# Gate and up of a fused AdaLN block on one core: from 2x2 block products of one pair to a 26-product 4x4 by 4x2 scheme over two pairs

## The chip, the cores and the metric

One core of one Trainium2 chip runs the whole program in one launch. The metric is device time in microseconds (us) of that core, and the time of a kernel is the median of its runs. Of the kernel before there are three: 2610.93, 2619.89 and 2622.31 us, so the median is 2619.89 us.

## The reference, cut to what matters

x is 2 x 2048 x 1024 and the feed-forward width is 2752. The attention is across the two batch entries only, so it is cheap; nearly all arithmetic lies in the three weight matrices.

```python
h = layernorm(x) * (1 + ca) + sa
x = x + ga * attention_over_the_2_batch_entries(h)
h = layernorm(x) * (1 + cb) + sb
gate = silu(h @ W_gate.T)       # W_gate, W_up: 2752 x 1024
up = h @ W_up.T
x = x + gb * ((gate * up) @ W_down.T)   # W_down: 1024 x 2752
```

## The kernel before, in words

**Tiling.** The tokens are cut into eight units of 2 x 256 (512 columns). A unit runs in three stages. *Gate and up* makes H = silu(gate) * up, 21 blocks of 128 rows and one of 64, taken as ten pairs of blocks (p = 0 to 9), a single block (p = 10) and a left-over of 64 rows (`gu_left_over`, L1034). *Down* multiplies by W_down in seven steps of 120 matmuls (L1166). Then eight groups of five matmuls add the last rows of W_down (`pB`, L1196). `unit` does one unit; the loop at the end of the program does eight.

**Precision.** An f32 operand is held as two f16 parts, high and low. A product is three matmuls (`PARTS`): high by high, high by low, low by high. `split` makes the two parts: ScalarE writes the high one (L168), VectorE the low one (L172), as source times scale minus high. Scales are powers of two found from sums of squares (L151).

**Fewer products.** Gate-and-up of one pair is a 2x2 by 2x2 block product: rows are gate and up, the inner side is two halves of the 1024 inputs, columns are the two batch entries. `gu_pair` (L996) does it in 7 products in place of 8, after Strassen and Winograd, in the order `GU_STEPS`, with three PSUM accumulators X, Y, Z, each in two buffers. VectorE and ScalarE put the results together: L1001, L1004, L1007, L1010, L1013, L1014, L1016, L1018, L1019, L1022, L1023. `gu_as_is` (L964) does the 8 plain products. The seven left operands of a pair are sums of its four weight blocks.

**Where left operands are built.** The first unit uses plain f16 blocks (`gu_plain`, L939, matmuls of 512 columns) and stores them to DRAM (`dgu`). In the second unit the odd pairs and p = 10, in the third the even pairs, are built from f32 weights loaded again (`Stream`, `operand`; sums at L447 to L452) and used at once, and stored for later. The even pairs run plain in the second unit. From the fourth unit on all seven operands are loaded from `dgu`.

**Right operands.** `right_gu` makes eight right operands of the next unit's h (four blocks, four sums) with copies of 1024 columns on ScalarE (L899) and sums on VectorE (L900 to L913), beside the last three down steps.

**The next unit's h.** `prep(u + 1)` is a generator (`side`): loads, attention, layer norm. Its VectorE lines are L687, L688, L703, L704, L706, L713, L719, L159 to L162 and L731. GpSimd sums over partitions twice in it (L694). `unit` calls it between steps.

**What sets the order.** Loads and stores are issued by SyncE, in one queue. Engines work in order. From the second unit on a list scheduler lays out each engine's order when the program is built; it moves instructions of all engines, matmuls too, where their operands allow it. `tc.issue_after` and the places of the `yield`s hold it back. PSUM has eight banks: X, Y, Z twice, and two for small things. `rot` (five blocks of 1024 columns) holds the right operands of two down steps in turn, and in the second and third units also the f32 weights that operands are built from.

**Other lines that are spoken of.** L166 is a high part made by GpSimd, and L132 a maximum over partitions on GpSimd; both are in the first unit. L841 is a sum of 512 columns on GpSimd before the first unit.

Of the kernel before, what the change touches and what calls it, by code (L numbers as in the profile page):

```python
# [16 lines left out]
P = 128  # L17
# [22 lines left out]
GU_STEPS = (("X", 1), ("Y", 6), ("Z", 5), ("X", 2), ("Y", 7), ("Z", 3), ("Y", 4))  # L40
DN_STEPS = (("X", 1), ("Z", 5), ("Y", 6), ("X", 2), ("Y", 7), ("Z", 3), ("Y", 4))
LAST = ((0, 0, 0), (0, 0, 1), (0, 1, 0), (1, 0, 0), (1, 1, 0))
PARTS = ((0, 0), (0, 1), (1, 0))
# [3 lines left out]
def adaln_kernel(ctx, tc, x, xT, wgp, wg20, wgl, wd, wd20, wd21, wmod, cT, out, nunits=NU):  # L47
# [23 lines left out]
    ets = {"sil": [0, 1], "e1": [2, 3], "e5": [4]}  # L71
    bct = ct([P, 2, 2, TU], "bct")
    hb = hbt.bitcast(F16).rearrange("p (o h k c) -> p o h k c", o=8, h=2, k=4)
    rot16 = rot.bitcast(F16).rearrange("p (s h k c) -> p s h k c", s=2, h=2, k=KH)
    zt = big[:, 2].rearrange("p (k n c) -> p k n c", k=KB, n=2)
    flat = lambda t: t.rearrange("p a b -> p (a b)")

    def et_tile(tag):

        i = ets[tag].pop(0)  # L80
        ets[tag].append(i)
        return mix[:, 3 * D + i * 2 * TU:3 * D + (i + 1) * 2 * TU].rearrange("p (n c) -> p n c", n=2)
# [291 lines left out]
    def x_step(s, between):  # L374
# [32 lines left out]
        for n in range(2):  # L407
# [10 lines left out]
    AS_IS = range(0, NP, 2)  # L418
    PAIRS = {1: list(range(NP + 1)), 2: [p ^ 1 for p in range(NP)] + [NP]}
    BUILT = {1: [p for p in PAIRS[1] if p not in AS_IS], 2: list(AS_IS)}  # L420
    dgu = {(p, i): dr.tile([P, 2 * min(2, NF - 2 * p) * 4 * P], F16, tag=f"dgu{p}_{i}", name=f"dgu{p}_{i}")
           for p in range(NP + 1) for i in range(0 if p in AS_IS else 1, 8)}
# [9 lines left out]

    ORDER = [i for _, i in GU_STEPS]
    BLOCKS = (1, 2, 0, 4)
    PLAIN = {1: 0, 2: 1, 4: 3}
    AHEAD0, AHEAD1 = 3, 4
# [18 lines left out]
    class Pair:  # L455
# [49 lines left out]
        def store(self, i, w):  # L505
            if i != 2 or self.p in AS_IS:
                Q.dma_start(dgu[self.p, BLOCKS[i]], w)

        def operand(self, i):
            w = self.w[i] = wtile(2 * self.n, "wo")  # L510
            split(w[:, 0:self.n], w[:, self.n:], combine(self.q, i), self.s)
            Q.dma_start(dgu[self.p, i], w)

    class Stream:


        def __init__(self, u):
            self.items = [(p, i) for p in PAIRS[u] for i in (range(4) if self.as_is(u, p) else ORDER)]
            self.u, self.to_build, self.w, self.n, self.src = u, list(BUILT[u]), {}, 0, {}
            self.at = 0  # L520

        @staticmethod
        def as_is(u, p):
            return u == 1 and p in AS_IS

        def next_source(self):
            if self.to_build:
                p = self.to_build.pop(0)
                self.src[p] = Pair(p, ring(self.n))
                self.n += 1  # L530
                self.src[p].load()

        def make(self, k):
            while self.at <= min(k, len(self.items) - 1):
                p, i = self.items[self.at]
                self.at += 1
                if p in BUILT[self.u] and i not in PLAIN:
                    self.src[p].operand(i)
                    self.w[p, i] = self.src[p].w.pop(i)
                    if i == 3:  # L540
                        self.next_source()
                else:
                    w = self.w[p, i] = wtile(2 * min(2, NF - 2 * p) * 4 * P, "wo")
                    Q.dma_start(w, dgu[p, BLOCKS[i] if self.as_is(self.u, p) else i])

    NXT = 3
    FROM, EVERY = 8, {1: 2, 2: 2}
# [11 lines left out]

    def ring(p):  # L560

        at = lambda j: rot[:, j % 6 * D:(j % 6 + 1) * D] if j % 6 < 5 else hpf
        return [at(4 * p + j) for j in (0, 3, 1, 2)]
# [329 lines left out]


    def right_gu(E):
        b11, b12, b21, b22 = (zt[:, 4 * i:4 * i + 4, n] for i in range(2) for n in range(2))

        def op(i, src):
            S.copy(hb[:, i, 0], src)  # L899
            V.tensor_tensor(hb[:, i, 1], src, hb[:, i, 0], ALU.subtract)  # L900

        op(1, b11)
        E.tensor_tensor(b11, b12, b11, ALU.subtract)
        yield
        op(5, b11)
        E.tensor_tensor(b11, b22, b11, ALU.subtract)
        yield
        op(6, b11)
        op(2, b21)
        yield  # L910
        E.tensor_tensor(b21, b21, b11, ALU.subtract)
        op(0, b12)
        E.tensor_tensor(b12, b22, b12, ALU.subtract)  # L913
        yield
        op(7, b12)
        op(3, b22)
        yield
        op(4, b21)
        yield
# [32 lines left out]
    def gu_as_is(p, ws, asq, tick):  # L952

        inv = inv_f[:, p:p + 1]
        pt = {(m, f): ps.tile([P, 2, TU], F32, tag="XYZ"[(4 * p + 2 * m + f) % 3], name=f"g{m}{f}")
              for m in range(2) for f in range(2)}
        for i in range(4):
            m, kh = i // 2, i % 2
            w = ws(i).rearrange("p (h f k c) -> p h f k c", h=2, f=2, k=4)
            for f in range(2):  # L960
                for k in range(4):
                    for j, (wa, ha) in enumerate(PARTS):
                        for n in range(2):
                            T.matmul(pt[m, f][:, n], w[:, wa, f, k], hb[:, ((1, 0), (2, 3))[kh][n], ha, k],  # L964
                                     start=kh == 0 and k == 0 and j == 0 and n == 0,
                                     stop=kh == 1 and k == 3 and j == 2, skip_group_check=True)
            if kh:
                for f in range(2):
                    if m == 0:
                        sil = evp.tile([P, 2, TU], F32, tag="ev", name="silp", bufs=3)  # L970
                        S.activation(sil, pt[m, f], AF.Silu, scale=inv)
                        pt["s", f] = sil
                    else:
                        mark["pair", p] = V.scalar_tensor_tensor(H[:, 2 * p + f], pt[m, f], inv, pt["s", f], ALU.mult, ALU.mult)
            tick(i)
        sumsq(H[:, 2 * p:2 * p + 2].rearrange("p f n c -> p (f n c)"), asq[:, p:p + 1])
# [7 lines left out]
    def gu_pair(u, p, ws, asq, tick):  # L984
        nf = min(2, NF - 2 * p)
        acc = {a: ps.tile([P, 2, TU], F32, tag=a, name=f"p{a}") for a in "XYZ"}
        pt = {a: acc[a][:, 0:nf] for a in "XYZ"}
        inv = inv_f[:, p:p + 1]
        et = lambda tag: (evp.tile([P, 2, TU], F32, tag=tag, name=tag, bufs=3) if tag == "ev" else et_tile(tag))[:, 0:nf]
        seen = set()  # L990
        for si, (a, i) in enumerate(GU_STEPS):
            w = ws(i).rearrange("p (h f k c) -> p h f k c", h=2, f=nf, k=4)
            for f in range(nf):
                for k in range(4):
                    for j, (wa, ha) in enumerate(PARTS):
                        T.matmul(pt[a][:, f], w[:, wa, f, k], hb[:, i, ha, k], start=a not in seen,  # L996
                                 stop=k == 3 and j == 2, skip_group_check=True)
                        seen.add(a)
            if si == 0:
                e1 = et("e1")  # L1000
                S.copy(e1, pt["X"])  # L1001
            if si == 1:
                u2 = et("ev")
                V.tensor_tensor(u2, pt["Y"], e1, ALU.add)  # L1004
            if si == 2:
                e5 = et("e5")
                S.copy(e5, pt["Z"])  # L1007
            if si == 3:
                sl = et("sil")
                S.activation(sl, pt["X"], AF.Silu, scale=inv)  # L1010
            if si == 4:
                c22 = et("ev")
                V.tensor_tensor(c22, pt["Y"], e1, ALU.add)  # L1013
                V.tensor_tensor(c22, c22, e5, ALU.add)  # L1014
            if si == 5:
                V.tensor_tensor(u2, pt["Z"], u2, ALU.add)  # L1016
                sr = et("sil")
                S.activation(sr, u2, AF.Silu, scale=inv)  # L1018
                V.scalar_tensor_tensor(H[:, 2 * p:2 * p + nf, 1], c22, inv, sr, ALU.mult, ALU.mult)  # L1019
            if si == 6:  # L1020
                c21 = et("ev")
                V.tensor_tensor(c21, pt["Y"], e1, ALU.add)  # L1022
                mark["pair", p] = V.scalar_tensor_tensor(H[:, 2 * p:2 * p + nf, 0], c21, inv, sl, ALU.mult, ALU.mult)  # L1023
            tick(si)
        sumsq(H[:, 2 * p:2 * p + nf].rearrange("p f n c -> p (f n c)"), asq[:, p:p + 1])

    def gu_left_over(u, w, asq, between=lambda: None):
        pl = ps.tile([P, 2, TU], F32, tag="X", name="pl")
        w = w.rearrange("p (h k c) -> p h k c", h=2, k=KB)
        for n in range(2 if u else 1):  # L1030
            for k in range(KB):
                o = ((1, 0), (2, 3))[k // 4][n]
                for j, (wa, ha) in enumerate(PARTS):
                    T.matmul(pl[:, n] if u else pl.rearrange("p n c -> p (n c)"), w[:, wa, k],  # L1034
                             hb[:, o, ha, k % 4] if u else hb0[:, ha, k], start=n == 0 and k == 0 and j == 0,
# [3 lines left out]
        sl = et_tile("sil")  # L1039
# [7 lines left out]
    def unit(u, side, nxt):  # L1047
# [34 lines left out]
        taken, before = 0, None  # L1082
        for p in PAIRS.get(u, range(NP + 1)):
            if u == 0:
# [7 lines left out]
            elif u in streams:  # L1092
                st = streams[u]

                def tick(si):
                    nonlocal taken
                    taken += 1
                    st.make(taken + AHEAD1)
# [510 lines left out]
```

## Time and profile before, and how to read it

| | |
|---|---|
| median of three runs | 2619.89 us |
| the profiled execution: time | 2618.47 us |
| its span, first to last instruction | 2616.3 us |
| TensorE, share of the span | 97% |
| VectorE, ScalarE, GpSimd | 61%, 37%, 4% |
| DMA | 586.61 MB, mean 224 GB/s |
| start of the last-rows stage (`pB`) of the eight units | 465.7, 791.0, 1097.9, 1397.9, 1701.5, 2001.8, 2305.0, 2603.9 us |

Units are numbered 1 to 8 here. The time from one `pB` to the next is one unit: its `pB`, then gate-and-up and down of the following one. So 465.7 to 791.0 is the period of the second unit (325.3 us), and so on. In a row of groups the two numbers after the bar are busy time in us and mean length of one in ns; then follow the idle time ahead of it and what ended that. A line of the timeline has start, length, engine, line, operation; "x2" are two instructions in a row.

### The profile page before, as it was taken

The page shows a single profiled execution, that of the slowest core. Times are in us where ns is not written, and L with a number is a line of the kernel's source. Part 1 is how long each engine was busy: PE and PEld are TensorE (multiplying, and loading weights), DVE is VectorE, ACT ScalarE, POOL GpSimd, SP SyncE. Part 2 cuts the span into 40 slices and gives each one's busy share as a digit, 9 for nine tenths or more (in the row PEclk, how much of TensorE's full clock was granted, in tenths as well). Part 3 has the DMA queues.
Part 4 walks back from the last instruction along what each step waited for, and adds up shares of the span by engine and source line. Part 5 has one row for each costly group of instructions (what it writes and reads, how often), then busy time and mean ns, then how long its engine had stood idle before and what let it go on. Part 6 is the DMA issues. An engine that isn't in the chain of part 4 may idle for free.

```text
span 2616.3 us, 50450 instructions
## 1 busy us (share of the span) xinstructions
PE 2543.5 (97%) x21699; PEld 2089.9 (80%) x21699; DVE 1588.7 (61%) x2616; ACT 978.8 (37%) x1402; POOL 114.1 (4%) x68
## 2 busy tenths in 40 slices
PE   7899969999999999999999999999999999999999
PEld 3344448788887888888887888888887888888887
DVE  8778697565767777592376625584284725622263
ACT  7667764233432454152241423233141412311231
POOL 6200000000000000000000000000000000000000
PEclk9999989999999999999999999999999999999999
DMA  9978756755568766676666666676666666666664
GB/s 391 395 282 317 290 205 207 263 171 199 176 214 286 262 214 211 204 232 202 200 200 226 201 202 200 197 237 201 186 219 219 198 201 200 202 197 202 202 203 156
DMA packets 154976, 586.61 MB, mean 224 GB/s; under 512 B 16768, under 2 KB 16832, under 8 KB 154752
## 3 DMA queue, kind: packets, MB, share of 16 engines
q1 hardware_dynamic: 154752, 583.38, 67.3%
q8 instruction: 170, 2.79, 0.4%
q14 instruction: 54, 0.44, 0.1%
HBM read 506.47 MB, written 76.84 MB: 223 GB/s over the span
## 4 chain that ended last, share of the span: by engine, by line
PE 81%; DMA 7%; DVE 6%; ACT 2%; issue 2%; POOL 0%; SPq 0%; DVEq 0%; ACTq 0%; POOLq 0%
PE pY L996 19%; PE pZ L996 12%; PE dY L1166 12%; PE pX L996 12%; PE dZ L1166 8%; PE dX L1166 8%; PE g L964 3%; PE g L939 2%; PE pB L1196 2%; DMA wo<-dgu 1%; PE pl L1034 1%; DMA out_dram<-big 1%; DVE bst L289 1%; DMA rot<-in_wgp_dram 1%; DMA wl<-dgl 1%
## 5 line engine op out<-in xcount | busy, mean ns | idle before, releaser
L996 PEld LDWEIGHTS <-w 128*128 128x128 f16 x8820 | 864.2, 98 | 113.0 <-DMA w<-dgu 8.3
L1166 PEld LDWEIGHTS <-wd 128*128 128x128 f16 x6720 | 658.2, 98 | 82.2 <-issue 5.6
L996 PE MATMUL pY<-hbt,w 128*128 128x256 f16 x3780 | 444.0, 273 | 0.0
L1166 PE MATMUL dY<-rot,wd 128*128 128x256 f16 x2880 | 318.6, 273 | 0.0
L996 PE MATMUL pZ<-hbt,w 128*128 128x256 f16 x2520 | 295.9, 273 | 7.2 <-DMA w<-dgu 7.2
L996 PE MATMUL pX<-hbt,w 128*128 128x256 f16 x2520 | 300.6, 273 | 0.0
L996 PEld LDWEIGHTS <-wo 128*128 128x128 f16 x2688 | 263.9, 98 | 41.7 <-DMA wo<-dgu 7.4
L168 ACT ACTIVATE rot<-H,sA 128x1024 f16<-128x1024 f32 x168 | 162.3, 1001 | 235.7 <-PE dY L1166 126.9
L172 DVE SCALAR_TENSOR_TENSOR rot<-H,sA,rot 128x1024 f16<-128x1024 f32 x168 | 182.7, 1101 | 81.9 <-ACT rot L168 81.5
L939 PE MATMUL g<-hbt,wq 128*128 128x512 f16 x1008 | 221.1, 381 | 8.3 <-DVE wq L172 3.6
L1166 PE MATMUL dX<-rot,wd 128*128 128x256 f16 x1920 | 214.7, 274 | 4.9 <-issue 4.9
L1166 PE MATMUL dZ<-rot,wd 128*128 128x256 f16 x1920 | 214.7, 273 | 0.1
L1013 DVE TENSOR_TENSOR ev<-pY,mix 128x512 f32<-128x512 f32 (+1 forms) x72 | 47.8, 663 | 257.8 <-PE pY L996 256.7
L939 PEld LDWEIGHTS <-wq 128*128 128x128 f16 x1008 | 98.3, 98 | 132.5 <-issue 7.5
L151 ACT ACTIVATE junk<-H 128x1024 bf16<-128x1024 f32 (+1 forms) x102 | 100.8, 988 | 177.5 <-DVE H L1023 149.6
L1018 ACT ACTIVATE mix<-ev,inv_f 128x512 f32<-128x512 f32 (+1 forms) x72 | 50.4, 701 | 248.2 <-DVE ev L1016 247.6
L996 PE MATMUL pY<-hbt,wo 128*128 128x256 f16 x1152 | 135.8, 274 | 2.7 <-DMA wo<-dgu 1.3
L702 ACT ACTIVATE o<-big,beta,alpha 128x256 f32<-128x256 f32 x96 | 51.5, 593 | 194.8 <-DVE big L688 181.7
L1004 DVE TENSOR_TENSOR ev<-pY,mix 128x512 f32<-128x512 f32 (+1 forms) x72 | 47.7, 662 | 123.9 <-PE pY L996 123.9
L1007 ACT COPY mix<-pZ 128x512 f32<-128x512 f32 (+1 forms) x72 | 40.4, 561 | 190.6 <-PE pZ L996 190.6
L1147 DVE SCALAR_TENSOR_TENSOR big<-dY,cA,big 128x256 f32<-128x256 f32 x96 | 41.9, 478 | 113.7 <-PE dY L1166 113.7
L964 PE MATMUL g<-hbt,wo 128*128 128x256 f16 x960 | 108.1, 275 | 2.3 <-DMA wo<-dgu 2.3
(331 smaller groups left out, 2734.4 us busy)
## 6 DMA issues: line engine op xcount, KB each, us to landing
w<-dgu SPq DMA_DIRECT2D x350, 512.0 KB, 4.2
wd<-dwd SPq DMA_DIRECT2D x224, 640.0 KB, 5.1
wo<-dgu SPq DMA_DIRECT2D x85, 512.0 KB, 5.4
dgu<-wo SPq DMA_DIRECT2D x40, 512.0 KB, 3.9
rot<-in_wgp_dram SPq DMA_DIRECT2D x38, 512.0 KB, 5.9
dgu<-wq SPq DMA_DIRECT2D x35, 512.0 KB, 6.5
dwd<-hbt SPq DMA_DIRECT2D x28, 640.0 KB, 3.3
out_dram<-big SPq DMA_DIRECT2D x30, 512.0 KB, 3.8
```

The lines of the kernel that those rows point to most:

```text
L151: S.activation(jv, src, AF.Square, accum_out=col)
L168: mark["hi"] = S.activation(dst_hi, src, AF.Copy, scale=s)
L172: return V.scalar_tensor_tensor(dst_lo, src, s, dst_hi, ALU.mult, ALU.subtract)
L702: S.activation(o[:, n], z[:, q, 0], AF.Identity, scale=alpha[:, n, 0, q:q + 1], bias=beta[:, n, q:q + 1])
L939: T.matmul(pt[m, f].rearrange("p n c -> p (n c)"), w[:, wa, f, k], hb0[:, ha, 4 * kh + k], start=kh == 0 and k == 0 and j == 0, stop=kh == ...
L964: T.matmul(pt[m, f][:, n], w[:, wa, f, k], hb[:, ((1, 0), (2, 3))[kh][n], ha, k], start=kh == 0 and k == 0 and j == 0 and n == 0, stop=kh ...
L996: T.matmul(pt[a][:, f], w[:, wa, f, k], hb[:, i, ha, k], start=a not in seen, stop=k == 3 and j == 2, skip_group_check=True)
L1004: V.tensor_tensor(u2, pt["Y"], e1, ALU.add)
L1013: V.tensor_tensor(c22, pt["Y"], e1, ALU.add)
L1018: S.activation(sr, u2, AF.Silu, scale=inv)
L1166: T.matmul(acc[a, h][:, j], w[:, k // 5, wa, k % 5], rot16[:, si % 2, ha, k], start=(a, h) not in seen, stop=k == KH - 1 and jj == 2, skip ...
L1196: T.matmul(pB, wt[:, k, wa, m, :], hp[:, k, ha, :], start=i == 0, stop=i == len(LAST) - 1)
```

## The change

- The first unit stores all four plain blocks of every pair (before, the third block of the odd pairs and of p = 10 was not stored).
- The second unit does all ten pairs plain (`gu_as_is`), and p = 10 too. Beside it a generator, `build`, makes the left operands of all five groups of two pairs: per group 35 sums of 512 columns, two of three on GpSimd and the third on VectorE, and 26 splits of 512 columns, each stored to DRAM (`dq`, 256 KB). It loads all f32 weights again. Its f32 blocks lie in `rot` and in the second half of `hbt`, 16 registers of 512 columns and one more, and three for temporary sums; the f16 results use five places in `mix`.
- From the third unit on `gu_group` does two pairs at a time: gate and up of two pairs are four rows, the 1024 inputs four quarters, the batch entries two columns. 26 products of 2 x 2 x 3 matmuls stand in place of 2 x 7 products of 2 x 4 x 3. It uses six accumulators (all six banks of X, Y, Z), 22 sums and 4 products on VectorE and 6 copies and 4 silu on ScalarE in each group. p = 10 runs plain.
- `right_gu` makes 27 right operands of 512 columns with 21 sums (in the second unit the 8 plain ones). They lie in `hbt`, in `rot` (ten places, those of the two down buffers) and in one block of H.
- `Feed` loads left operands four tiles ahead, in their order of use, 512 KB each. `prep` is called at each tile in the second unit and at every fifth later.

The core of the diff:

```diff
-GU_STEPS = (("X", 1), ("Y", 6), ("Z", 5), ("X", 2), ("Y", 7), ("Z", 3), ("Y", 4))
+G_STEPS = (
+    (2, 4, True, (('c', 0),)),
+    (10, 2, True, (('c', 1),)),
+    (12, 3, True, (('c', 2),)),
+    (17, 4, False, (('+', 1, 1),)),
...
+    (19, 5, False, (('-', 2, 2), ('h', 2, 0, 0, 1),)),
+)
+G_LEFT = (
+    ('e', 13, 1, 1), ('e', 12, 4, 1), ('e', 17, 10, 1), ('o', 't', 12, '-', 0), ('e', 15, 't', 1),
+    ('o', 0, 0, '+', 1), ('o', 12, 12, '-', 0), ('o', 't', 0, '-', 10), ('e', 2, 't', 1), ('o', 't', 12, '+', 9),
...
+)
+    def build():
...
+        for i in range(8):
+            load(0, i)
+        nt = ns = na = 0
+        for q in range(NQ):
+            last = None
+            for at, x in enumerate(G_LEFT):
+                reg = lambda r: last if r == "t" else regs[r]
+                if x[0] == "o":
...
+                    na += 1
+                    E = V if na % 3 == 0 else G
+                    E.tensor_tensor(dst, reg(a), reg(b), ALU.add if sign == "+" else ALU.subtract)
...
+                    w = place(ns % 5).bitcast(F16).rearrange("p (h f c) -> p h f c", h=2, f=2)
+                    s = s_q[:, int(sign < 0), q:q + 1]
+                    split(w[:, 0], w[:, 1], reg(src), s)
+                    j = at_of[r]
+                    Q.dma_start(dq[q, j // 2][:, j % 2 * NL:(j % 2 + 1) * NL], w.rearrange("p h f c -> p (h f c)"))
+                for i, e in ends.items():
+                    if e == at and q + 1 < NQ:
+                        load(q + 1, i)
+                if x[0] == "e":
+                    yield
...
+    def gu_group(q, take, asq, tick):
+        inv = inv_q[:, q:q + 1]
+        acc = [ps.tile([P, 2, TU], F32, tag="XYZ"[i % 3], name=f"p{i}") for i in range(6)]
+        e = [place(i).rearrange("p (f c) -> p f c", f=2) for i in range(5)]
+        e.append(evp.tile([P, 2, TU], F32, tag="ev", name="e", bufs=3))
+        for at, (r, a, first, reads) in enumerate(G_STEPS):
+            if at % 2 == 0:
+                w2 = take().rearrange("p (t h f k c) -> p t h f k c", t=2, h=2, f=2, k=2)
+            w, right = w2[:, at % 2], right_of(G_OPERAND[r])
+            for f in range(2):
+                for k in range(2):
                     for j, (wa, ha) in enumerate(PARTS):
+                        T.matmul(acc[a][:, f], w[:, wa, f, k], right[:, ha, k], start=first and f == 0 and k == 0 and j == 0,
+                                 stop=k == 1 and j == 2, skip_group_check=True)
+            for x in reads:
+                if x[0] == "c":
+                    S.copy(e[x[1]], acc[a])
...
+                else:
+                    sign, src, dst = x
+                    in0, in1 = (acc[a], e[src]) if sign == "r" else (e[src], acc[a])
+                    V.tensor_tensor(e[dst], in0, in1, ALU.add if sign == "+" else ALU.subtract)
+            tick()
...
+        def tick(*_):
+            nonlocal taken
+            taken += 1
+            if u == 1:
+                for _ in range(3 + taken % 3 // 2):
+                    run_gen(builder)
+                if taken > 5:
+                    run_gen(side)
+            elif taken % 5 == 0:
+                run_gen(side)
...
+            if u == 1:
+                builder = build()
+                for p in range(NP):
+                    gu_as_is(p, feed.take, asq, tick)
+                for _ in builder:
+                    pass
             else:
+                for q in range(NQ):
+                    gu_group(q, feed.take, asq, tick)
+            close_scale(0, 0, NP)
+            gu_as_is(NP, feed.take, asq, tick)
...
-                if si >= 4:
-                    with tc.issue_after(mark["lo", NXT].ins), tc.issue_after(mark["hi", NXT].ins):
-                        run_gen(nxt)
-                        run_gen(nxt)
+                if si >= READY:
+                    with tc.issue_after(mark["lo", READY].ins), tc.issue_after(mark["hi", READY].ins):
+                        for _ in range((5, 6, 5, 5)[si - READY]):
+                            run_gen(nxt)
```

## The prediction

> **What bounds the kernel now.** First the page: busy time, the slices, the chain.
>
> ```profile
> PE 2543.5 (97%) x21699; PEld 2089.9 (80%) x21699; DVE 1588.7 (61%) x2616; ACT 978.8 (37%) x1402; POOL 114.1 (4%) x68
> ...
> DVE  8778697565767777592376625584284725622263
> ...
> PE 81%; DMA 7%; DVE 6%; ACT 2%; issue 2%; POOL 0%; SPq 0%; DVEq 0%; ACTq 0%; POOLq 0%
> ```
>
> TensorE is never free for long and makes 81% of the chain; VectorE swings between 2 and 9 tenths. Then the stretches from one `pB` to the next, one unit each (columns: stretch, its length, busy time of PE, weight loads, DVE, ACT, POOL, clock, DMA share, GB/s), and one piece of the chain.
>
> ```profile
> 465.70:791.00 325.30, 316.99 (x2818) 277.36 (x2817) 207.47 (x300) 111.47 (x161) 6.48 (x2) 0.98 0.61 204
> 791.00:1097.90 306.90, 301.31 (x2698) 264.31 (x2696) 215.28 (x317) 116.09 (x167) 6.47 (x2) 0.99 0.70 236
> 1097.90:1397.90 300.00, 298.98 (x2698) 263.73 (x2697) 171.13 (x277) 94.66 (x147) 6.47 (x2) 1.00 0.67 208
> ...
> 2305.00:2603.90 298.90, 298.80 (x2698) 263.76 (x2696) 111.33 (x179) 62.99 (x94) 0.00 (x0) 1.00 0.62 193
> ```
>
> ```profile
> 2551.52 13.10 PE dX L1166 x120
> ```
>
> 120 matmuls of 256 columns take 13.10 us: 0.1092 us each, 0.2184 for 512 columns. A unit from the third on has 1764 + 48 + 840 of them and 40 of 512 columns: 2652 x 0.1092 + 8.7 = **298.3 us**, against 298.9 to 306.9 measured. Only fewer matmuls can shorten such a unit. The second has 1884 in place of 1764: 311.4, so 13.9 of its 325.3 are idle.
>
> **Matmuls.** From the third unit on, 10 pairs x 168 + 84 become 5 groups x 26 x 12 + 96 = 1656: 108 fewer, 11.8 us; the floor is 286.5 us. Six units: -70.8. The second goes from 1884 to 10 x 192 + 96 = 2016: +14.4, floor 325.9. TensorE alone would save 56.4 us.
>
> **The build in the second unit.** Five groups x 35 sums are 175, of which 117 fall to GpSimd and 58 to VectorE; 130 splits. Prices:
>
> ```profile
> L841 POOL TENSOR_TENSOR big<-o,big 128x512 f32<-128x512 f32 x5 | 6.3, 1274 | 3.2 <-DVE o L840 3.2
> ```
>
> ```profile
> 1144.56 4.90 DVE L713 TENSOR_TENSOR big<-big,mean 128x512 f32<-128x512 f32 x8
> ...
> 1170.22 6.41 DVE L731 SCALAR_TENSOR_TENSOR big<-big,b1s,r 128x256 f32<-128x256 f32 x16
> ```
>
> ```profile
> 1326.99 1.40 DVE L172 SCALAR_TENSOR_TENSOR mix<-H,sA,mix 128x512 f16<-128x512 f32 x2
> ```
>
> In a row, VectorE takes 0.61 us for a sum of 512, 0.40 for the 256-column form, 0.70 for a split. So GpSimd: 117 x 1.274 = 149.1, and 2 x 3.2 for the sums over partitions = **155.5**. VectorE: 130 x 0.70 + 58 x 0.61 = 126.4; `prep` 46 x 0.61 + 32 x 0.40 + 2 = 42.9; together **169.3**, plus 21 plain results x 0.745 = 15.6. Either fits beside TensorE's 225.4 us (2016 + 48 matmuls). Whether both do depends on what happens when they meet. Four lines of one place, GpSimd and VectorE side by side:
>
> ```profile
> 134.05 1.12 POOL L166 TENSOR_SCALAR wq<-rot,s_gu 128x1024 f16<-128x1024 f32 x1 [18.62 <-DVE inv_gu L139]
> 135.81 1.49 POOL L166 TENSOR_SCALAR wq<-rot,s_gu 128x1024 f16<-128x1024 f32 x1 [0.64 <-DMA dgu<-wq]
> ```
>
> ```profile
> 135.02 3.34 DVE L172 SCALAR_TENSOR_TENSOR wq<-rot,s_gu,wq 128x1024 f16<-128x1024 f32 x2 [0.91 <-ACT wq L168]
> 138.64 1.28 DVE L172 SCALAR_TENSOR_TENSOR wq<-rot,s_gu,wq 128x1024 f16<-128x1024 f32 x1 [0.27 <-ACT wq L168]
> ```
>
> Alone, the GpSimd instruction takes 1.12 and two splits 2 x 1.28 less an overlap of 0.08 = 2.48. Overlapping, they take 1.49 and 3.34: GpSimd loses 0.37, VectorE 0.86 us. Likewise a VectorE sum meets the sum over partitions here:
>
> ```profile
> 1139.65 3.23 POOL L694 PARTITION_ALL_REDUCE mean<-acc  x1 [210.07 <-DVE acc L706]
> ...
> 1140.47 1.98 DVE L1014 TENSOR_TENSOR ev<-ev,mix 128x512 f32<-128x512 f32 x1
> ```
>
> 1.98 in place of about 0.69. In both, VectorE reads two operands from SBUF. L841's neighbours (L840) read one from PSUM, and L841 keeps 1.27. Splits, VectorE's sums and `prep` all read two from SBUF. If such an instruction and a GpSimd one exclude each other, the two totals add: 155.5 + 169.3 = **325 us**, 99 over TensorE. If GpSimd only holds VectorE up for 0.86 of its 1.12 (77%), 117 x 1.274 x 0.77 = 115, and the sum is 290. If they don't hinder each other, 225.4 and the 13.9 idle us of before. I take 325: the lines with two SBUF operands are the ones like the build's.
>
> The Trainium skill, "GPSIMD Engine Reference", section Specifications, says that GpSimd's SBUF interfaces are shared with VectorE, with contention from VectorE instructions that have two SBUF inputs. By L841's row alone this stage would last 225 us; by the page's rule, read as exclusion, 325; no run here shows a long series of both.
>
> Upper bound: add four changes of GpSimd's work between plain sums and sums over partitions, in a program with both (its first p2g waited 6.5 us for nothing that the profile shows: 26 us), and four reloads of f32 blocks between groups, since a group's last steps use blocks that the next group's first steps want (5.9 us median to landing, 24 us): 375.
>
> TensorE can't run away from it: VectorE works in order and writes H between the build's instructions, and the first down operand overwrites the build's `rot`. That operand (L168, L172: 1.15 + 1.28) is then late by some 3 us. Second unit: 325 + 3 + 91.7 (down) + 8.7 = **428, +103** over 325.3. Ends: +14 (225.4 + 13.9 + 100.4 = 339.7) and +153.
>
> DMA: 80 MB (21 plain blocks, 21 f32, 34 stores, the rest small), 247 GB/s over 325 us, against 391 in the page's densest slices; at 225 us it would be 356 and no longer loose. Stores queue ahead of weights on SyncE, but four loaded tiles are 4 x 48 x 0.109 = 21 us ahead.
>
> **Third to eighth unit.** VectorE gets 5 x (22 + 4) results, 16.4 us a group (22 x 0.61 + 4 x 0.745), and 48 steps for right operands, 29.3 us, for 14.6 before (12 x 1.22, the row of L900). In the down stage VectorE sat idle for most of 1361 to 1398, which takes the latter; the last few wait for `rot` and fall into the first group, which doesn't need them at once. In the groups, the built program's order puts nearly all of `prep` (42.9 and reciprocals 3.4) into the first two: 2 x 16.4 + 41 (less 5.3 that stand earlier) = 73.8 us beside 2 x 34.1 = 68.2 of matmuls. All six accumulators are one group's; where VectorE lags, TensorE waits. I take 5 us for the difference and 5 for the next group's first copies, which stand behind the last products and the sums of squares (1.06 each) on ScalarE: **10 us** idle. Ends: 1.7 (the third to seventh stretch's best) and 20 (`prep` at the rows' means, 0.69 and 0.48, and once more the 5). The eighth has no `prep`: 4.
>
> Third: 296.5 - 306.9 = -10.4. Fourth to seventh: 4 x 296.5 - 1207.1 = -21.1. Eighth: 290.5 - 298.9 = -8.4. Sum **-40**; ends -84 and +10.
>
> **At nothing.** The first unit's 6 more stores (under 4 MB beside half-idle DMA; 2 us if the cover is gone), its shorter right operands (-9 us of VectorE off the path), the scales (a few 0.15 us).
>
> **Sum**, against the profiled execution (2618.5: its span and 2.2 us around it that stay; 1.4 below the median): 2618.5 + 103 - 40 = **2682 us**. If the build's sum is 290: 2647. With everything at its upper end: 2618.5 + 153 + 10 = 2782; at its lower: 2618.5 + 14 - 84 = 2549.
>
> **Rivals.**
> - *Faster: the build hides.* GpSimd and VectorE share without loss, each 70 to 85% busy, and gate-and-up of the second unit stays at 239. For it: each total is below 225.4, and L841. 2618.5 + 14 - 40 = **2593**; with the best idle times 2549. It decides from a build under 262 us, where +40 in the second unit equals the -40 later.
> - *About the same: exclusion in part.* Some meetings cost, splits go on while GpSimd waits for a sum of VectorE; build 265 to 275: +43 to +53, -40: **2627**.
> - *Slower still: the order binds.* One group's 61 steps are a chain, GpSimd waits for VectorE's third sum and both for reloaded blocks; build 375: +153, -40, so **2732**, and to 2782 if the groups also starve.
> - That the product isn't done as said is excluded: the built program has 516 matmuls fewer, 132 x 1 - 108 x 6.
>
> **How the numbers follow.** Forecast (build 290 to 350) 0.60; hidden 0.18; in part 0.11; order binds 0.11. The range reaches down to the hidden case's 2593 and up past 2732: 2590 to 2745, with about 0.09 below and 0.06 above. By half a per cent (about what a measurement here can tell from no change), faster is below 2606.8 (0.18), the same up to 2633 (0.10), slower above (0.72). The likeliest case's own range is 2647 to 2707.
>
> **What would show it.** Right: gate-and-up of the second unit near 325 us, with TensorE waiting for VectorE's results there; GpSimd sums and VectorE splits longer than 1.27 and 0.75 where they overlap; later periods near 296 us; each later idle gap ended by VectorE or ScalarE at a group's border. Wrong: overlapping sums and splits at their lone lengths, a second unit near 340 us, or later periods that don't fall below 300.

## The result, and the profile after

The changed kernel takes **2708.66 us**, the median of four runs (2704.33 to 2718.33), against 2615.41 us for the kernel before in the same measurement: ratio 1.0363, 95% interval 1.0317 to 1.0409. It is slower, and the forecast of 2682 was 27 us too low. The profiled execution took 2718.33 us, 9.7 above the median; its span is 2716.5.

From its page, busy time, the slices of GpSimd, the granted clock (in tenths of full speed) and the chain:

```profile
PE 2522.0 (93%) x21183; PEld 2050.5 (75%) x21183; DVE 1970.7 (73%) x3224; ACT 1080.0 (40%) x1631; POOL 305.6 (11%) x185
...
POOL 6200100536750010001000010001000000000000
PEclk9999989988879999999999999999999999999999
...
PE 58%; DMA 7%; DVE 5%; POOL 2%; issue 2%; ACT 1%; POOLq 0%; SPq 0%; DVEq 0%; ACTq 0%
```

TensorE issues 516 matmuls fewer and is busy 21 us less, but its share of the span falls from 97% to 93%. GpSimd is busy in five slices of the second unit, and there TensorE's granted clock is lowest. The stretches from one `pB` to the next (second, third and eighth unit):

```profile
466.30:903.30 437.00, 349.71 (x2951) 297.70 (x2950) 356.02 (x437) 172.50 (x268) 194.19 (x119) 0.90 0.65 224
903.30:1205.90 302.60, 291.53 (x2589) 254.41 (x2587) 219.88 (x368) 106.19 (x173) 6.80 (x2) 0.99 0.57 195
...
2414.80:2703.90 289.10, 287.55 (x2590) 252.98 (x2588) 149.42 (x240) 68.83 (x104) 0.00 (x0) 1.00 0.55 188
```

The periods of all units, in us, from the start of one `pB` to that of the next in each profiled execution. The columns e1 to e9 are experiments, told of below; those of e5, e8 and e10 that matter are given there.

| unit | before | after | e1 | e2 | e3 | e4 | e7 | e9 |
|---|---|---|---|---|---|---|---|---|
| 2 | 325.3 | 436.9 | 387.7 | 451.9 | 435.4 | 389.6 | 341.9 | 341.5 |
| 3 | 306.9 | 302.7 | 301.3 | 303.3 | 290.7 | 294.1 | 302.7 | 300.9 |
| 4 | 300.0 | 301.8 | 302.4 | 301.7 | 291.7 | 294.0 | 294.1 | 292.5 |
| 5 | 303.4 | 302.9 | 302.7 | 303.0 | 292.4 | 295.0 | 294.3 | 291.1 |
| 6 | 300.3 | 301.0 | 300.2 | 303.8 | 291.3 | 294.7 | 296.5 | 293.2 |
| 7 | 303.3 | 303.1 | 300.1 | 303.5 | 291.1 | 292.7 | 294.1 | 290.1 |
| 8 | 298.9 | 289.1 | 289.3 | 288.7 | 288.7 | 288.7 | 289.6 | 288.8 |

Two things happened. The second unit grew by 111.6 us. And of the six units that have fewer matmuls, only the eighth, the one in which no next h is made, became shorter as its matmuls did (-9.8); the five between gained 2.4 us together.

**The second unit.** Groups of GpSimd and VectorE in its gate-and-up:

```profile
L644 POOL TENSOR_TENSOR rot<-rot 128x512 f32<-128x512 f32 x31 | 50.2, 1624 | 35.8 <-DVE rot L644 15.5 <-DVE mix L245 11.0 <-DVE acc L826 7.1
```

```profile
L245 DVE SCALAR_TENSOR_TENSOR mix<-rot,s_q,mix 128x512 f16<-128x512 f32 x51 | 60.2, 1183 | 9.7 <-ACT mix L241 9.7
...
L1078 DVE SCALAR_TENSOR_TENSOR H<-g,inv_f,silp 128x512 f32<-128x512 f32 x21 | 15.5, 740 | 0.0
L810 DVE SCALAR_TENSOR_TENSOR o<-big,alpha,o 128x256 f32<-128x256 f32 x16 | 15.4, 980 | 0.0
```

These are the largest groups of each kind. GpSimd's sums take 1.62 us in theirs (1.58 over all 115 in the stretch from 475.0 to 795.9) where L841 of the kernel before took 1.27. VectorE's splits take 1.18 (1.09 over all 121 there) for 0.75, and the 256-column step of the next h (L810) 0.98 for 0.48. The results that read one operand from PSUM (L1078) keep their 0.74. TensorE, meanwhile, waits for weights, near the end of gate-and-up once for VectorE, and SyncE for the splits that its stores want (in such a line: us in total, times, longest):

```profile
PE g L1068 <- DMA wg<-dgu: 58.6, 11, 18.0
PE pa L185 <- DVE p2b L196: 15.2, 1, 15.2
```

```profile
SPq L654 <- DVE mix L245: 189.5, 109, 17.7
```

**The later units.** What TensorE waited for in the fourth, and what VectorE and ScalarE did at the first long gap (TensorE stood until 1223.77, for L1105):

```profile
PE p L1101 <- DMA wg<-dq: 5.6, 5, 2.7
PE p L1101 <- ACT mix L1105: 2.5, 1, 2.5
PE p L1101 <- DVE mix L1115: 1.7, 1, 1.7
```

```profile
1219.39 1.29 DVE L794 TENSOR_TENSOR big<-big,bct 128x512 f32<-128x512 f32 x2 [2.23 <-DMA big<-in_xT_dram]
1220.60 0.87 DVE L1281 SCALAR_TENSOR_TENSOR big<-pB,cB,big 128x256 f32<-128x256 f32 x2
1221.38 1.28 DVE L795 TENSOR_TENSOR big<-big,bct 128x512 f32<-128x512 f32 x2
```

```profile
1222.16 1.09 ACT L809 ACTIVATE o<-big,beta,alpha 128x256 f32<-128x256 f32 x2 [1.59 <-DVE big L795]
1223.16 0.56 ACT L1105 COPY mix<-p 128x512 f32<-128x512 f32 x1
```

L794, L795 and L809 are steps of the next unit's h. They stand ahead of the last additions of the unit before (L1281), whose store then leaves late, and ahead of the copy L1105, which frees an accumulator.

### The profile page after: what moved, and what is told of

It is laid out like the page before. It is cut to its first block, busy times and chain, and to the rows that moved or that the text cites. A ratio compares the mean times of both kernels' runs of the same rounds, so it can differ in the third digit from the quotient of the medians.

```text
span 2716.5 us, 50838 instructions
## 1 busy us (share of the span) xinstructions
PE 2522.0 (93%) x21183; PEld 2050.5 (75%) x21183; DVE 1970.7 (73%) x3224; ACT 1080.0 (40%) x1631; POOL 305.6 (11%) x185
## 4 chain that ended last, share of the span: by engine, by line
PE 58%; DMA 7%; DVE 5%; POOL 2%; issue 2%; ACT 1%; POOLq 0%; SPq 0%; DVEq 0%; ACTq 0%
PE p L1101 30%; PE dY L1251 10%; PE dZ L1251 7%; PE dX L1251 7%; DMA wg<-dq 5%; PE g L1068 2%; PE pB L1279 1%; PE pl L1126 1%; DVE big L838 1%; DVE mix L1115 1%; POOL rot L644 1%; DMA out_dram<-big 1%; DMA big<-in_xT_dram 1%; DVE mix L245 0%; DMA dq<-mix 0%
## 5 line engine op out<-in xcount | busy, mean ns | idle before, releaser
L1101 PEld LDWEIGHTS <-wg 128*128 128x128 f16 x9360 | 919.4, 99 | 188.5 <-DMA wg<-dq 49.2
L1101 PE MATMUL p<-hbt,wg 128*128 128x256 f16 x5040 | 602.8, 275 | 33.1 <-DMA wg<-dq 24.3
L1115 DVE TENSOR_TENSOR mix<-mix,p 128x512 f32<-128x512 f32 x540 | 360.6, 683 | 286.8 <-PE p L1101 238.4
L1101 PE MATMUL p<-rot,wg 128*128 128x256 f16 x3960 | 476.8, 274 | 25.0 <-DMA wg<-dq 13.6
L1068 PE MATMUL g<-hbt,wg 128*128 128x256 f16 x2592 | 303.9, 281 | 61.1 <-DMA wg<-dgu 58.6
L1068 PEld LDWEIGHTS <-wg 128*128 128x128 f16 x2592 | 260.9, 101 | 102.3 <-DMA wg<-dgu 64.7
L1105 ACT COPY mix<-p 128x512 f32<-128x512 f32 x180 | 102.2, 581 | 270.2 <-PE p L1101 250.5
L1107 ACT ACTIVATE mix<-mix,inv_q 128x512 f32<-128x512 f32 x90 | 61.7, 717 | 117.0 <-DVE mix L1115 117.0
L1107 ACT ACTIVATE e<-e,inv_q 128x512 f32<-128x512 f32 x30 | 21.7, 723 | 198.7 <-DVE e L1115 198.7
L1111 DVE SCALAR_TENSOR_TENSOR H<-mix,inv_q 128x512 f32<-128x512 f32 x90 | 77.0, 860 | 18.9 <-ACT mix L1107 16.1
L809 ACT ACTIVATE o<-big,beta,alpha 128x256 f32<-128x256 f32 x96 | 52.4, 593 | 69.9 <-DVE big L811 58.5
L1115 DVE TENSOR_TENSOR e<-e,p 128x512 f32<-128x512 f32 x90 | 61.4, 682 | 19.4 <-PE p L1101 17.4
```

What stands on the lines that cost most here:

```text
L809: S.activation(o[:, n], z[:, q, 0], AF.Identity, scale=alpha[:, n, 0, q:q + 1], bias=beta[:, n, q:q + 1])
L1068: T.matmul(pt[m, f][:, n], w[:, wa, f, k], plain_of(2 * kh + k // 2, n)[:, ha, k % 2], start=kh == 0 and k == 0 and j == 0 and n == 0, sto ...
L1101: T.matmul(acc[a][:, f], w[:, wa, f, k], right[:, ha, k], start=first and f == 0 and k == 0 and j == 0, stop=k == 1 and j == 2, skip_group ...
L1105: S.copy(e[x[1]], acc[a])
L1107: S.activation(e[x[1]], e[x[1]], AF.Silu, scale=inv)
L1111: V.scalar_tensor_tensor(H[:, 2 * p:2 * p + 2, n], e[u], inv, e[s], ALU.mult, ALU.mult)
```

## The experiments

**All sums on VectorE (e1), all on GpSimd (e2).** One line each.

```diff
-                    E = V if na % 3 == 0 else G
+                    E = V        # e1
+                    E = G        # e2
```

> All 175 sums of the build go to VectorE, none to GpSimd; nothing else changes. Theory A (VectorE and GpSimd hinder each other, so that the build's two shares nearly add): VectorE then has 130 x 0.70 + 175 x 0.61 + 46 for the next unit's h + 15.6 for plain results = 259 us in the second unit's gate-and-up, GpSimd only its 6.5; sums and splits fall back to 0.61 to 0.75 us; gate-and-up is bound by VectorE alone at 260 to 280 us instead of about 340, the second unit's period is 355 to 380 instead of 437.0, the whole about 2630 to 2655. Rival B (no hindrance; the second unit is long because weight loads queue on SyncE behind stores that wait for splits): 117 sums more on VectorE are 71 us more ahead of the splits, the period stays at 437 or grows. Rival C (GpSimd's reloaded blocks and its changes between sums and sums over partitions bind): the period falls by at most 26 to 50 us.

> All 175 sums of the build go to GpSimd, none to VectorE; nothing else changes. Theory A: GpSimd has 175 x 1.274 + 6.5 = 229.5 us, VectorE 130 x 0.70 + 46 + 15.6 = 153; if the two add, gate-and-up of the second unit is 382 us and its period some 475 to 485 instead of 437.0; with sums of 1.5 to 1.8 us as they were measured beside VectorE, 263 to 315 us of GpSimd alone. Rival B or no hindrance: GpSimd's 229.5 us lie beside VectorE's 153, gate-and-up about 240 to 260 and the period 340 to 360.

e1: 2664.68 us, median of four, ratio to the kernel before 1.0188 (1.0171 to 1.0205); 44.0 less than the change, though VectorE got 117 instructions more. e2: 2735.05 us, one run. From e1, the second unit's window, its VectorE sums, and the waits of TensorE and SyncE in it:

```profile
468.80:856.40 387.60, 337.44 (x2950) 293.10 (x2948) 340.16 (x554) 173.43 (x268) 8.64 (x2) 0.92 0.73 253
```

```profile
L644 DVE TENSOR_TENSOR rot<-rot 128x512 f32<-128x512 f32 x53 | 36.0, 682 | 0.1
```

```profile
PE dX L1251 <- ACT rot L241: 20.6, 1, 20.6
PE dZ L1251 <- ACT rot L241: 12.3, 1, 12.3
...
PE g L1068 <- DMA wg<-dgu: 6.2, 2, 5.3
```

```profile
SPq L654 <- DVE mix L245: 164.4, 110, 6.7
```

The sums are back at 0.68. SyncE still waits 164 us for splits, but TensorE waits 6.2 us for weights instead of 58.6. Rival B wanted the period to stay or grow; it fell by 49. That lies in rival C's 26 to 50 too, and e1 by itself doesn't decide against it, since it takes away both the meetings of the two engines and GpSimd's changes of work; e6 and e10 below part them. The period missed the upper end of my 355 to 380 by 8 us. Gate-and-up itself ended after 243.9 us, before my 260 to 280, because part of the build went on beside the down stage: VectorE alone is the bound now (busy for 340 of the 387.6 us), and the operands of the first two down steps stand behind what is left of its work. e2 went the way of theory A (+15), but not by the 38 to 48 us of full addition: its GpSimd sums took 1.4 to 1.7 us by group and the period is 451.9. Why it fell that far short stays open.

**The two engines alone and side by side (e6).** A program with no other work, of this kind; in `meet` both engines wait for each other:

```diff
+    for f, n, g in ((None, 0, 24), (v_sum, 32, 0), (v_sum, 64, 24), (v_split, 32, 0), (v_split, 64, 24), (v_psum, 32, 0),
+                    (v_psum, 64, 24), (v_one, 32, 0), (v_one, 64, 24)):
+        meet()
+        for i in range(max(n, g)):
+            if i < n:
+                f(i)
+            if i < g:
+                g_sum(i)
```

> None of the block's arithmetic is done, zeros are stored: series of 128x512 instructions alone and side by side. 24 GpSimd sums alone, then 32 VectorE instructions alone and 64 beside 24 GpSimd sums, for four kinds of VectorE instruction: sum of two SBUF operands, split (two SBUF operands, 16-bit result), sum with one operand in PSUM, product with a scalar (one SBUF operand). Last four times sum, sum, sum over partitions, sum on GpSimd alone. Theory A by full exclusion: 64 x 0.61 + 24 x 1.27 = 69.5 us for the sums side by side, 64 x 0.70 + 30.5 = 75 for the splits, against 39 and 45 if they don't hinder each other; with one operand in PSUM or one operand at all no loss, 39 to 45. Changes between sums and sums over partitions: a gap of 6 to 8 us at each change if the 6.7 and 8.2 us of the second unit are their price, none if not.

VectorE's timeline (sum, split, one operand in PSUM, product with a scalar; each 32 alone, then 64 beside GpSimd), then GpSimd's (24 alone, then beside each of the four, then the first of four sums over partitions):

```profile
43.34 19.35 DVE L135 TENSOR_TENSOR vo<-va,vb 128x512 f32<-128x512 f32 x32
...
63.45 64.07 DVE L135 TENSOR_TENSOR vo<-va,vb 128x512 f32<-128x512 f32 x64
...
128.16 21.29 DVE L138 SCALAR_TENSOR_TENSOR vl<-va,one,vh 128x512 f16<-128x512 f32 x32
...
150.09 66.67 DVE L138 SCALAR_TENSOR_TENSOR vl<-va,one,vh 128x512 f16<-128x512 f32 x64
...
217.41 19.21 DVE L141 TENSOR_TENSOR vo<-va,pt 128x512 f32<-128x512 f32 x32
...
237.25 38.34 DVE L141 TENSOR_TENSOR vo<-va,pt 128x512 f32<-128x512 f32 x64
...
276.25 12.75 DVE L144 TENSOR_SCALAR vo<-va,one 128x512 f32<-128x512 f32 x32
...
289.63 49.58 DVE L144 TENSOR_SCALAR vo<-va,one 128x512 f32<-128x512 f32 x64
```

```profile
13.33 29.32 POOL L147 TENSOR_TENSOR go<-ga,gb 128x512 f32<-128x512 f32 x24
...
63.30 39.59 POOL L147 TENSOR_TENSOR go<-ga,gb 128x512 f32<-128x512 f32 x24
...
150.06 39.63 POOL L147 TENSOR_TENSOR go<-ga,gb 128x512 f32<-128x512 f32 x24
...
237.22 29.50 POOL L147 TENSOR_TENSOR go<-ga,gb 128x512 f32<-128x512 f32 x24
...
289.60 33.50 POOL L147 TENSOR_TENSOR go<-ga,gb 128x512 f32<-128x512 f32 x24
...
348.00 3.25 POOL L167 PARTITION_ALL_REDUCE go<-ga  x1 [5.70 <-issue]
358.24 3.69 POOL L147 TENSOR_TENSOR go<-ga,gb 128x512 f32<-128x512 f32 x3 [6.98 <-issue]
```

Lone, 64 VectorE sums are 2 x 19.35 = 38.7 us and 24 GpSimd sums 29.3; side by side they end after 64.07, against 68.0 if they exclude each other and 38.7 if they don't. For splits it is 66.67 against 71.9 and 42.6. So exclusion holds to 6 or 7%. While both run, 24 GpSimd sums take 39.6 us (1.65 each). VectorE then has 64.07 - 39.6 = 24.5 us alone, enough for 40.5 sums; so it gets through 23.5 in the 39.6 us, one for each of GpSimd's. With one operand in PSUM there is no loss on either side (38.34 against 2 x 19.21, 29.50 against 29.32). I expected none with one operand at all, and that was wrong: the product with a scalar, 0.40 us alone, needs 49.6 us for 64 in place of 25.5 (54.8 by full exclusion). The Trainium skill, "SBUF — State Buffer", section "Who interferes with whom", states both: two SBUF inputs, or a two-port mode such as a product with a scalar can enter, take a port pair that GpSimd shares, an exclusive lock; at most one SBUF input outside those modes does not. These runs agree on which of the four kinds collide; in time, the exclusion measured is 6 to 10% short of full.

Each of the four changes from plain sums to a sum over partitions costs GpSimd 5.7 to 6.0 us, and each change back 7.0 to 7.3.

**Without the sums over partitions (e10).**

```diff
-            G.partition_all_reduce(t, acc, P, bass_isa.ReduceOp.add)
+            if u == 2:
+                V.tensor_copy(t, acc)
+            else:
+                G.partition_all_reduce(t, acc, P, bass_isa.ReduceOp.add)
```

> The changed kernel, in which the two sums over partitions in the second unit are left out (a copy on VectorE in their place, so the next unit's normalisation is another): GpSimd then has only plain sums there. Alone, such a sum takes 3.25 us and the two changes around it 5.8 and 7.1 us. Theory A (GpSimd is on the path of the build nearly always): the second unit's period falls by 20 to 32 us from 437. Rival (VectorE works on while GpSimd changes, and nothing is lost): by 8 us or less.

The second unit's period fell from 436.9 to 414.0 us (2699.10 in all, one run). So 23 of the 2 x 3.25 + 2 x (5.8 + 7.1) = 32 us that GpSimd is freed of had been on the path. (The other runs that leave the second unit's work as it is, e3, e5 and e8, have periods of 434.6 to 437.2, so 23 us is far more than the scatter.)

**The stores off SyncE's queue (e8).** Each store of a built operand is issued by ScalarE, two results late.

```diff
-                    Q.dma_start(dq[q, j // 2][:, j % 2 * NL:(j % 2 + 1) * NL], w.rearrange("p h f c -> p (h f c)"))
+                    pend.append((dq[q, j // 2][:, j % 2 * NL:(j % 2 + 1) * NL], w.rearrange("p h f c -> p (h f c)")))
...
+                            S.dma_start(*pend.pop(0))
```

> The stores of the built operands are issued from ScalarE's queue, each two results late, so that weight loads and reloads on SyncE no longer stand behind them. Theory A (VectorE and GpSimd set the end of the build, TensorE's 58.6 us of waiting for weights only show where its idle time falls): second unit 427 to 447 us, as now. Rival B (that queue is what makes the unit long): 437 - 58.6 = 378 us, the whole 2650.

The period stayed at 437.2 (2721.52 in all, one run). That is what theory A said, but the edit did less than it was meant to: the reloads of f32 blocks stayed in SyncE's queue and waited for VectorE and GpSimd there (the longest 24.7 us), so TensorE still waited for weights:

```profile
PE g L1072 <- DMA wg<-dgu: 51.9, 11, 22.2
```

So e8 doesn't show what a free queue would be worth. e1 bears on it: there the stores are still in that queue and SyncE waits nearly as long in total (164.4 us, but never more than 6.7 at once), and the weights are in time.

**The next h held to its place (e3).** From the third unit on, a step of the next h may not stand ahead of the reading that it was called after.

```diff
-                    V.tensor_tensor(e[dst], in0, in1, ALU.add if sign == "+" else ALU.subtract)
+                    mark["gv"] = V.tensor_tensor(e[dst], in0, in1, ALU.add if sign == "+" else ALU.subtract)
...
             elif taken % 5 == 0:
-                run_gen(side)
+                with tc.issue_after(mark["gv"].ins), tc.issue_after(mark["ga"].ins):
+                    run_gen(side)
```

(`ga` is ScalarE's last copy or silu of the group, marked in the same way.)

> From the third unit on, each step of the next unit's h may not stand ahead of the group reading it was called after, on VectorE and on ScalarE; in the built order its VectorE instructions then are 18, 20, 14, 10 and 23 beside the five groups instead of 47, 21, 17, 0 and 0. Its loads on SyncE may move as before. Theory A (the next h crowds VectorE beside the first two groups, and TensorE waits for accumulators there): units three to seven, 301 to 303 us now, fall to 292 to 297 each, the whole by 30 to 45 us to 2665 to 2680. Rival B (weight tiles come late because SyncE's queue stands at loads of x that wait for the previous output to be stored): no change beyond 2 us a unit, the whole within 10 us of 2708.

2666.54 us, ratio 1.0196 (1.0181 to 1.0211): 42.1 less than the change. The fifth unit, and TensorE's waits in it:

```profile
1484.40:1776.80 292.40, 287.86 (x2591) 252.78 (x2589) 219.35 (x368) 105.10 (x173) 6.47 (x2) 1.00 0.63 202
```

```profile
PE p L1101 <- DMA wg<-dq: 3.6, 5, 1.7
PE p L1101 <- DVE mix L1115: 0.9, 1, 0.9
```

VectorE does the same 219 us of work, but units three to seven fall to 290.7 to 292.4, 54.3 us less in the two profiled executions. (By the medians the gain is 42.1; of the 13 us between, 9.7 are the changed kernel's profiled execution above its median and 3.7 that of e3 below its own.) More than half of the waits for weights went too, with the loads left free to move: 36.3 us in units three to seven of the changed kernel, 16.2 in e3. Which of the two engines' orders matters more was not tried.

**Only the loads held (e5).**

```diff
             elif taken % 5 == 0:
-                run_gen(side)
+                with tc.issue_after(mark["gq"].ins):     # the last weight tile asked for
+                    run_gen(side)
```

> Only the loads of the next unit's x are held on SyncE, behind the weight tiles that were asked for before them; VectorE and ScalarE keep the order of the changed kernel. Theory A (VectorE crowded beside the first two groups makes the late output stores and late weight tiles too): units three to seven stay at 300 to 303 us, the whole within 12 us of 2708. Rival B (the queue order on SyncE is the cause): the periods fall to 296 or less, the whole by 30 us or more.

2721.46 us, one run; units three to seven 302.3 to 304.0. Nothing is gained, and the waits turn from weights to VectorE. In the fourth unit:

```profile
PE p L1101 <- DVE mix L1115: 6.7, 5, 2.8
PE p L1101 <- DMA wg<-dq: 4.7, 5, 1.9
PE p L1101 <- DVE e L1115: 3.4, 2, 1.9
```

So the order on VectorE and ScalarE makes most of the loss, and the late tiles are in good part a consequence: over units three to seven the waits for weights are 36.3 us in the changed kernel, 23.0 with the loads held and 16.2 with that order changed. What makes the rest of them late is open.

**Both edits (e4), and the last group built in the third unit (e7, e9).** e4 is e1 with e3 and e5. e7 adds that the second unit builds four groups, and the third takes the last two pairs plain and builds the fifth group beside them. The builder gets three steps a tile there and, in the second unit, two or three instead of three or four; the next h is called at every fourth product of the third unit instead of the fifth. e9 is e7 with the loads left free.

```diff
+                builder = build(range(NQ - 1))
...
+                for q in range(NQ - 1 if u == 2 else NQ):
                     gu_group(q, feed.take, asq, tick)
+                if u == 2:
+                    builder = build([NQ - 1])
+                    for p in (NP - 2, NP - 1):
+                        gu_as_is(p, feed.take, asq, tick)
```

> Both edits at once: all sums of the build on VectorE, and from the third unit on the next unit's h held to its place on VectorE, ScalarE and SyncE. If the two losses are separate, they add: 2708.7 - 44.0 - 42.1 = 2622.5 us, second unit 388, third to seventh 290 to 293 each. If they are one (VectorE merely short over the whole program), less than both: 2640 or more.

> As with both edits, and the second unit builds four groups of two pairs; the third unit takes the last two pairs as plain products and builds the fifth group beside them and the single block. VectorE is relieved of 35 x 0.61 + 26 x 0.67 = 39 us in the second unit: 388 - 39 = 349, if VectorE still sets its end, and no lower than 340 by TensorE's floor. The third unit gets 72 matmuls more, 7.9 us, and perhaps 5 us for a late first down operand: 291 + 13 = 304. Sum 2622.5 - 39 + 13 = 2596 us. Rival (the fifth group does not fit beside 528 plain matmuls, 57.7 us, since its blocks can only be loaded when the groups are done): third unit 320 or more, the whole 2612 or more.

> As the kernel that builds its last group in the third unit, but the loads on SyncE are no longer held. Held on VectorE and ScalarE alone, units three to seven took 290.7 to 292.4 us; with the loads held too, 292.7 to 295.0. If the held loads cost this, units four to seven fall from 294 to 297 to 291 to 293 each, and the whole from 2592 to about 2580. If not, 2592 again.

e4: 2628.86 us, ratio 1.0052 (1.0036 to 1.0069), 6.4 more than the sum of the two gains; its later units are 2 to 3 us longer than e3's. e7: **2592.17 us**, ratio 0.9916 (0.9901 to 0.9931). e9: **2582.58 us**, ratio 0.9875 (0.9857 to 0.9893). Second, third and fourth unit of e9:

```profile
465.30:806.80 341.50, 329.65 (x2951) 289.69 (x2949) 300.70 (x493) 156.10 (x242) 8.64 (x2) 0.98 0.75 255
806.80:1107.70 300.90, 295.97 (x2663) 260.04 (x2661) 241.60 (x407) 119.33 (x193) 6.82 (x2) 1.00 0.68 224
1107.70:1400.20 292.50, 289.17 (x2591) 253.76 (x2589) 219.24 (x368) 105.13 (x173) 6.47 (x2) 0.99 0.63 202
```

With 39 us less of VectorE's work the second unit comes to 341.5, 15.6 above TensorE's floor of 325.9, and its granted clock back to 0.98. The fifth group fits beside the plain pairs: the third unit costs 72 matmuls and a few us. Holding the loads as well had cost 9.6 us (e7 against e9). e9 is faster than both kernels: 1.2% below the one before (with the interval above, a small gain but clear of the scatter), 4.7% below the change.

## Why the prediction was right, and where it was not

The sign, the stage and the mechanism of the largest term were right: exclusion of GpSimd and VectorE in the second unit's build. The measured 2708.66 lies just above 2647 to 2707, the likeliest case's own range, since of the 31.5 us that units three to seven were to gain only 2.4 came. By its steps, in the profiled execution:

- **Matmuls**: right. The eighth unit, where nothing else competes, takes 289.1 (forecast 290.5, floor 286.5).
- **Gate-and-up of the second unit**, forecast 325: measured from the last of `pB` to the last left-over matmul, 320.9 (the build's last split ends at 812.9, in the down stage). The stretch and the down stage after it:

```profile
475.00:795.90 320.90, 244.53 (x2063) 209.02 (x2060) 266.85 (x297) 132.62 (x211) 188.61 (x117) 0.88 0.67 232
795.90:903.20 107.30, 96.38 (x843) 84.15 (x844) 83.82 (x129) 39.33 (x57) 5.10 (x3) 0.95 0.59 193
```

  The sum of 155.5 and 169.3 came out so well partly because two errors met. e6 shows exclusion to be 6 to 7% short of full addition, some 20 us; and e10 shows 23 us for the sums over partitions and the changes around them, of which I had 6.5 in the sum and 26 only in the upper end. That these two are all is worked out, not shown. By the two engines' timelines at least one of them is busy in 298 of the 320.9 us; in the other 23 neither is, and 14 of these lie in three gaps beside the two sums over partitions. The sign that I had named, TensorE waiting for VectorE's results, hardly shows: 58.6 of its waits there are for weights and 17.6 for VectorE. By these lines the build reaches TensorE mostly by way of SyncE's queue, whose stores wait for splits, and I had that path as harmless.
- **The first down operand**, forecast 3 us late: the down stage took 107.3 for 91.7, so 15.6. About 11 of it are waits for VectorE, ScalarE and weights; the rest is TensorE at a lower granted clock (0.95 in that row). Second unit: +111.6 measured, +103 forecast.
- **"DMA ... no longer loose", stores ahead of weights, 21 us of tiles ahead**: wrong as to the wait. TensorE waited 58.6 us for weights, once 18. Whether it cost anything by itself these runs don't show (e8 did not clear the queue). Against a cost: TensorE had 320.9 - 225.4 = 95 us to spare against the build, and most of the waits went when the build got shorter (e1). The end of the build (its last split, counted from the start of `pB`) also moves as the period does: 346.6 us in the changed kernel, 298.2 in e1, 362.7 in e2 and 325.5 in e10, so by -48, +16 and -21, where the periods moved by -49, +15 and -23.
- **Units three to eight**, forecast -40: this step failed in size. The prediction took 10 us of idle time in each of units three to seven, 5 for VectorE's crowding in the first two groups and 5 for the copies at group borders. The first is 10.9 on average (1511.5 us for the five units, less e3's 1457.2, over five). The second 5 agrees in size with what e3 leaves, 290.7 to 292.4 against 286.5, but by luck: there TensorE waits 2.7 to 3.8 us a unit for weights, at most 0.9 for VectorE and not for ScalarE's copies. In the changed kernel too most of the later gaps end with a weight tile (36.3 us of waits in five units), not with VectorE or ScalarE as I had said. I had compared totals, 73.8 us of VectorE's work with 68.2 of matmuls, which gives how far VectorE falls behind at the end of two groups. But readings stand in order among the steps of the next h from the first product on: a wait of such a step for its data delays them, as at 1219.39 above, and the output store and what stands behind it in SyncE's queue go late with them. The prices were low too: the changed kernel's page has 0.68 us for a reading sum (L1115) and 0.86 for a product (L1111), so a group takes 18.5 us in place of 16.4, and by my own formula, as an estimate, VectorE would lag by 9.7 us and not 5. How much is price and how much the waits in the order was not parted; e3 takes away both by moving the steps. Five units gained 2.4 us in place of 31.5.
- **Sum**: 2618.5 + 111.6 - 2.4 - 9.8 + 0.6 in the first unit = 2718.5. Of the 36 us above the forecast, 29 are units three to seven and 9 the second unit, less 1.4 in the eighth.
- **Rivals**: that the build hides is refuted by e1 and e6; "the order binds" has its changes of GpSimd's work (e10, 23 us), but its 375 us were not reached. Whether the chain of one group's 61 steps costs anything by itself was not tried; GpSimd stood idle 132 of the 320.9 us, mostly until a result of VectorE came, but VectorE worked through most of that, and, as far as the two exclude each other, only the 23 us in which neither was busy can be the chain's or the changes' alone. For reloaded blocks GpSimd waited only 5.0 us once the build had begun.

## What to carry to other kernels

Before work is given to an idle GpSimd, ask what VectorE does beside it: where its instructions read two operands from SBUF, the shares nearly add, and GpSimd needs 1.22 us for a sum that VectorE does in 0.61. Moving the 117 sums back, which also freed GpSimd of its changes of work, made this kernel 44 us faster. With fewer matmuls the engines that read the results must keep up in the right order: five units gave all but 2.4 of 59 us away, and 54 came back when the next unit's steps were held behind the readings. A build that overfills one stage can be cut where another stage has plain work to cover it.

## What was not expected of the hardware

- GpSimd pays for each change between plain sums and sums over partitions, and not only once: 5.7 to 6.0 us there, 7.0 to 7.3 back, four times in a row. The Trainium skill, "GPSIMD Engine Reference", section "2.1 Instruction dispatch", has about 6 us for the first call to a freshly loaded kernel, in its measurement the gap behind a `MODIFY_POOL_CONFIG`. In e6's trace each of the eight changes starts with two instructions of that name, so here it is paid at every change.
- A one-operand VectorE product at 0.40 us for 512 columns loses to GpSimd too (64 in 49.6 us for 25.5).
- After a wait TensorE is slow for a while. After the wait of 18 us in the changed kernel the granted clock stands at 0.50 and a matmul takes 0.21 us instead of 0.109; some 4 us later both are back. The first matmuls after the wait, and a later stretch (the clock is the third number from the end):

```profile
621.90:625.30 3.40, 3.39 (x17) 2.40 (x18) 3.40 (x10) 3.22 (x8) 0.00 (x0) 0.50 0.23 92
...
630.26:640.00 9.74, 9.61 (x88) 8.37 (x86) 9.74 (x9) 5.32 (x10) 7.23 (x5) 1.00 0.36 118
```
